# Attention with relative positions, one image at a time: products with v in groups of four key tiles, and x loaded late into a shared buffer

## The chip, the cores and the metric

The kernel runs on one core of one Trainium2 chip. The metric is the time of a run on the device in microseconds. Before the change the median of three runs was 2606.68 us (2600.14 to 2608.02).

## The reference

Eight images of 32 x 32 tokens (T = 1024) with 384 channels go through two layers. The change lies in the first one, cut here to what matters:

```python
# layer 0: x + attention(group_norm(x)), 6 heads of 64
qkv = (x @ qkv_w + qkv_b)                      # per image: q, k, v
attn = einsum('bqd,bkd->bqk', q * SCALE, k)    # 1024 x 1024 per head
attn = attn + rel_h[:, :, :, :, None] + rel_w[:, :, :, None, :]
attn = softmax(attn, axis=-1)
out = einsum('bqk,bkd->bqd', attn, v)
x = x + out @ proj_w + proj_b
# layer 1: t + causal-masked attention over layer_norm(t), then a feed-forward part
t = t + attn1(layer_norm(t))
t = t + ffn(layer_norm(t))
```

## The kernel before, in words

**Order of the whole.** The images are worked one after another. For each, `layer0` makes q, k and v from the group-normed input, the relative-position terms, and then the attention in `attend0_fast`. It returns the residual x and a function `more`, which finishes the projection. `attention1` (the second attention) and, for the first five images, the feed-forward part `ffn` follow. A second, general form of the program (`attend0_general`) stands behind a branch and isn't taken for these data.

**The attention of layer 0.** Scores are made transposed: keys lie on the 128 partitions, the 1024 queries along the free axis. The six heads go in three pairs (`p`), the two heads of a pair being `par` 0 and 1. The keys go in eight tiles of 128 (`c`). For each pair, tile and head, `scores` issues six matmuls (L554) into a PSUM tile of 128 x 1024: the product of k and q, that of the remainders of their rounding (`ks`), and the relative positions (`unit` with `r`), each for two halves of the queries. Their stationary tile is 128*128. ScalarE then takes the exponential into a page `pr` (L558). A page is a buffer of 128 x 1024 floats; a pool of eleven serves all pages, and a pool of eleven larger buffers of 128 x 3080 ("images") serves q, k, v, x and the like.

`values` works on the key tiles in `pending`. First VectorE adds each probability page to the running sum of its head (L567), for the denominator of the softmax. Then TensorE multiplies the probabilities with v (L572): four products per tile, one for each half of the queries and each head. A head has 64 channels, so a product uses 64 of the 128 columns (128*64): head 0 of the pair writes partitions 0 to 63, head 1 partitions 64 to 127. A product in full f32 leaves two records in the profile. Before the change `values` is called whenever two tiles are pending.

**What comes after a pair.** When pair p + 1 is at its second tile, `set_aside` copies the result of pair p to `oT` and folds its sums to 32 columns; at its tile c = 4, right after `values`, `divide` multiplies these into denominators (L602), takes the reciprocal (L580), spreads it (`wide`, L583), transposes it (`rb`, L585) and multiplies `oT` with it (L606). After the last pair `finish` does this without delay: the denominators come from the full sums by matmuls with a matrix of ones (L614), so TensorE needs the last sums of VectorE there; then a transpose (L617), the reciprocal and the spread as before, and a multiply (L620). The projection starts meanwhile on the first two pairs (L659) and is finished by `more` (L664), whose sum with x is on VectorE (L667).

**The residual x.** `residual` loads an image of x by four transfers of 384 KB on SyncE's queue (`load_x`, L105), and GpSimd adds the projection's bias `pb` in a single instruction over 128 x 3072 (L537). For the first image it is called when the binarizing of the feed-forward weights, which is woven into the attention of that image, has run out; in the trace that is in the last pair. For the others it is called at the first pair's second tile.

**What sets the order.** The program is written in the Tile framework. A scheduler with its own costs orders the instructions of each engine, and each engine then runs its own in that order. So the order on TensorE is not quite that of the code: products may be placed before or after a tile's scores, and a group of eight may be divided. The framework adds the waits that the buffers need. The group norm's input of the next image is loaded on SyncE's queue too (L307), behind x; two of the relative-position pages of each pair are worked by `split` (L506 on ScalarE, L507 on VectorE), the third pair's within the attention (`later`).

Of the kernel before, what the change touches and what calls it, by code (L numbers as in the profile page):

```python
# [13 lines left out]
ALU = mybir.AluOpType  # L14
# [3 lines left out]
P = 128  # L18
B, H, W, C = 8, 32, 32, 384
T = H * W  # L20
NJ = T // P
NC = C // P
NH, HD = 6, 64
NPAIR = NH // 2
# [50 lines left out]
def conv_attn_hybrid(  # L75
# [19 lines left out]
    nc = tc.nc  # L95
# [5 lines left out]
    def load_x(pools, b):  # L101
        t = pools.flat(f"x_{b}")[:, : NJ * C].rearrange("p (j c) -> p j c", j=NJ)
        src = x[b].rearrange("(j p) c -> p j c", p=P)
        for q in range(4):
            nc.sync.dma_start(out=t[:, 2 * q : 2 * q + 2, :], in_=src[:, 2 * q : 2 * q + 2, :])  # L105
        return t

    def tile_of(name, shape):
        return const.tile(shape, F32, name=name)
# [3 lines left out]
    pb, b2_sb = tile_of("pb", [P, C]), tile_of("b2_sb", [P, C])  # L113
# [179 lines left out]
    def stages(pools):  # L293
# [100 lines left out]
        def project(w, cols, xT, j, name):  # L394

            ps = pools.o_tile(name)
            for k in range(NC):
                nc.tensor.matmul(ps[:, :C], xT[:, k, ts(j, P)], w[:, k, cols], start=(k == 0), stop=(k == NC - 1))  # L398
            return ps[:, :C]
# [29 lines left out]
        def check(total, reciprocal, i):  # L429
            nc.vector.tensor_reduce(seen[:, 0, i : i + 1], total, AX.X, ALU.add)  # L430
            nc.vector.tensor_reduce(seen[:, 1, i : i + 1], reciprocal, AX.X, ALU.add)


        def layer0(b, xT):
# [99 lines left out]

            def residual():
                xt = load_x(pools, b)
                nc.gpsimd.tensor_tensor(xt, xt, pb.unsqueeze(1).to_broadcast([P, NJ, C]), ALU.add)  # L537
                return xt


# [4 lines left out]
        def attend0_fast(residual, b, sides, v, later):  # L545


            oT = pools.image(f"oT_{b}")

            def scores(p, c, par):  # L550
                sc = pools.s_tile(f"s0_{b}_{p}_{c}_{par}")
                for i, (keys, queries) in enumerate(sides[p][par]):
                    for half in range(2):
                        nc.tensor.matmul(  # L554
                            sc[:, half, :], keys[:, ts(c, P)], queries[:, ts(half, 512)], start=(i == 0), stop=(i == 2)
                        )
                pr = pools.page(f"pr0_{b}_{p}_{c}_{par}")
                nc.scalar.activation(pr, sc.rearrange("p a n -> p (a n)"), AF.Exp)  # L558
                return pr

            def values(p, chunks, sums, avs):
                for c, prs in chunks:
                    for par in range(2):
                        if c == 0:
                            continue
                        prev = first[par] if c == 1 else sums[par]
                        nc.vector.tensor_tensor(sums[par], prev, prs[par], ALU.add)  # L567
                for c, prs in chunks:
                    for half in range(2):
                        for par in range(2):  # L570
                            h = 2 * p + par
                            nc.tensor.matmul(  # L572
                                avs[half][ts(par, HD), :], v[:, c, ts(h, HD)], prs[par][:, ts(half, 512)],
                                start=(c == 0), stop=(c == NJ - 1),
                            )

            def reciprocals(p, tot):

                rt = pools.small.tile([P, 32], F32, tag="rt0", name=f"rt0_{b}_{p}")
                nc.vector.reciprocal(rt, tot)  # L580
                check(tot, rt, b * (NPAIR + 1) + p)
                wide = pools.page(f"wide0_{b}_{p}")
                nc.vector.tensor_copy(wide.rearrange("p (n i) -> p n i", i=32), rt.unsqueeze(2).to_broadcast([P, 32, 32]))  # L583
                rb = pools.page(f"rb0_{b}_{p}")
                nc.vector.transpose(rb, wide)  # L585
                return rb

            def set_aside(p, sums, avs):

                for half in range(2):  # L590
                    nc.scalar.copy(oT[:, p, ts(half, 512)], avs[half])
                few = pools.small.tile([P, 2, 32], F32, tag="few", name=f"few_{b}_{p}")
                for par in range(2):
                    tr = pools.page(f"tr0_{b}_{p}_{par}")
                    nc.vector.transpose(tr, sums[par])
                    nc.vector.tensor_reduce(few[:, par, :], tr.rearrange("p (n i) -> p n i", i=32), AX.X, ALU.add)
                return few

            def divide(p, few):
                den = pools.o_tile(f"den0_{b}_{p}")  # L600
                for par in range(2):
                    nc.tensor.matmul(  # L602
                        den[ts(par, HD), :32], fold.rearrange("p a i -> p (a i)"), few[:, par, :], start=True, stop=True
                    )
                rb = reciprocals(p, den[:, :32])
                nc.vector.tensor_tensor(oT[:, p, :], oT[:, p, :], rb, ALU.mult)  # L606

            def finish(p, sums, avs):

                tr = pools.page(f"tr0_{b}_{p}")  # L610
                for half in range(2):
                    den = pools.o_tile(f"den0_{b}_{p}_{half}")
                    for par in range(2):
                        nc.tensor.matmul(  # L614
                            den[ts(par, HD), :], ones, sums[par][:, ts(half, 512)], start=True, stop=True
                        )
                    nc.vector.transpose(tr[:, ts(half, 512)], den)  # L617
                rb = reciprocals(p, tr.rearrange("p (n i) -> p n i", i=32)[:, :, 0])
                for half in range(2):
                    nc.vector.tensor_tensor(oT[:, p, ts(half, 512)], avs[half], rb[:, ts(half, 512)], ALU.mult)  # L620

            xt, signs = None, binarize(pools) if b == 0 else None
            first = [None, None]
            for p in range(NPAIR):
                sums = [pools.page(f"sum0_{b}_{p}_{par}") for par in range(2)]
                avs = None
                pending = []
                for c in range(NJ):
                    prs = [scores(p, c, par) for par in range(2)]
                    if c == 0:  # L630
                        first = prs
                    if c == 1:
                        if p > 0:
                            few = set_aside(p - 1, *last)
                        if p == 0 and b > 0:
                            xt = residual()
                        avs = [pools.o_tile(f"av0_{b}_{p}_{half}") for half in range(2)]
                    if b == 0 and (p, c) >= (0, 1) and xt is None and next(signs, True):
                        xt = residual()
                    if len(pending) == 2:  # L640
                        values(p, pending, sums, avs)
                        if later:
                            later.pop()()
                        if c == 4 and p > 0:
                            divide(p - 1, few)
                        pending = []
                    pending.append((c, prs))
                values(p, pending, sums, avs)
                last = (sums, avs)
            finish(NPAIR - 1, *last)  # L650


            begun = []
            for j in range(4):
                if j % 2 == 0:
                    both = pools.s_tile(f"pj_{b}_{j}")
                begun.append(both[:, j % 2, :C])
                for k in range(2):
                    nc.tensor.matmul(begun[j], oT[:, k, ts(j, P)], wproj_sb[:, k, :], start=(k == 0), stop=False)  # L659

            def more(j):
                if j < 4:
                    ps = begun[j]
                    nc.tensor.matmul(ps, oT[:, 2, ts(j, P)], wproj_sb[:, 2, :], start=False, stop=True)  # L664
                else:
                    ps = project(wproj_sb, slice(0, C), oT, j, f"pj_{b}_{j}")
                nc.vector.tensor_tensor(xt[:, j, :], ps, xt[:, j, :], ALU.add)  # L667

            return xt, more
# [287 lines left out]
    with ExitStack() as scope:  # L957
        pools = Pools(scope, tc, "f")
# [43 lines left out]
```

## Time and profile before

| | before |
|---|---|
| median of the runs | 2606.68 us |
| profiled execution, span | 2599.5 us |
| granted TensorE clock, mean | 0.996 |
| busy: TensorE | 2521.0 us, 97% |
| busy: VectorE | 1619.4 us, 62% |
| busy: ScalarE | 1157.0 us, 45% |
| busy: GpSimd | 115.5 us, 4% |
| products with v, L572 | 1536 records, 359.7 us |
| scores, L554 (three groups) | 2304 records, 746.9 us |
| running sums, L567 (two groups) | 336, 406.9 us |
| adds of the bias to x, L537 | 8, 60.9 us, 7.6 us each |

In the profile PE stands for TensorE, DVE for VectorE, ACT for ScalarE, POOL for GpSimd and SP for SyncE. A group of instructions is given by its line, engine and operation and by the tiles that it writes and reads, with numbers left out of their names: `f_s` is a score tile, `f_av` a product with v, `f_pr` a page of probabilities, `f_sum` a running sum, `f_den` denominators, `f_x` an image of x. After the bar come the busy time and the mean of one instruction in nanoseconds, and then the idle time of the engine just before the group, with what ended it. The timeline view lists stretches of like instructions with their start, the time from first start to last end, and their number. Matmuls are pipelined and each record overlaps the next, so the time that one costs is read from start to start, not from its length.

### The profile page before, as it was taken

To read this page: it belongs to the slowest core of one execution; us is meant where nothing else is said; L and a number is where in the kernel's file an instruction comes from. 1 tells how busy PE (TensorE), PEld (TensorE's weight loads), DVE (VectorE), ACT (ScalarE), POOL (GpSimd) and SP (SyncE) were. 2 spreads that over 40 slices of the span, in tenths; PEclk is the share of its full clock that TensorE was granted. 3 is DMA by queue.
4 is the path that set the end of the run, shared out by engine and by line. 5 is a ranking of instruction groups with operands and counts; after the bars stand their busy time and mean duration, and the time that the engine had idled before them with its cause. 6 is when DMAs were issued, how large, how long until landed. Compare 5 with 4: busy or idle time off the path is not lost. (4 is left out here: it accounts for less than half of the span.)

```text
span 2599.5 us, 25162 instructions
## 1 busy us (share of the span) xinstructions
PE 2521.0 (97%) x9538; PEld 1508.4 (58%) x9538; DVE 1619.4 (62%) x2407; ACT 1157.0 (45%) x1513; POOL 115.5 (4%) x106
## 2 busy tenths in 40 slices
PE   7999998999999999999999999999999999999998
PEld 4555685555765556755557555576555555555554
DVE  5895468763587644786545776347864486538652
ACT  4641377421666314764127643156641264127420
POOL 1000002000001000010000100000100010001000
PEclk9999999999999999999999999999999999999999
DMA  6431106011042101150110601003200240015000
GB/s 167 147 146 61 37 1 170 1 61 37 1 117 54 49 13 37 41 130 1 61 37 1 170 1 61 6 31 91 80 25 1 67 104 1 25 39 131 1 1 26
DMA packets 148993, 144.72 MB, mean 56 GB/s; under 512 B 107264, under 2 KB 129664, under 8 KB 147328
## 3 DMA queue, kind: packets, MB, share of 16 engines
q1 hardware_dynamic: 142928, 119.36, 16.4%
q0 software_dynamic: 2880, 23.59, 2.6%
q8 instruction: 77, 1.26, 0.2%
q10 hardware_dynamic: 3056, 0.08, 0.1%
q14 instruction: 52, 0.43, 0.1%
HBM read 75.38 MB, written 42.47 MB: 45 GB/s over the span
## 5 line engine op out<-in xcount | busy, mean ns | idle before, releaser
L558 ACT ACTIVATE f_pr<-f_s 128x1024 f32<-128x1024 f32 x384 | 393.0, 1027 | 403.2 <-PE f_s L554 370.3
L567 DVE TENSOR_TENSOR f_sum<-f_sum,f_pr 128x1024 f32<-128x1024 f32 x288 | 349.0, 1244 | 147.0 <-ACT f_pr L558 145.6
L572 PE MATMUL f_av<-f_pr,f_v 128*64 128x512 f32 x1536 | 359.7, 599 | 0.0
L554 PE MATMUL f_s<-f_q,f_k 128*128 128x512 f32 x768 | 258.5, 418 | 21.8 <-ACT f_pr L558 14.9
L388 PE MATMUL f_qk<-f_gnT,wqkv_sb 128*128 128x512 f32 x576 | 261.5, 598 | 8.2 <-DVE f_k L456 5.6
L554 PE MATMUL f_s<-f_q,f_ks 128*128 128x512 f32 x768 | 245.3, 401 | 0.0
L554 PE MATMUL f_s<-f_r,unit 128*128 128x512 f32 x768 | 243.1, 398 | 0.0
L572 PEld LDWEIGHTS f_av<-f_pr,f_v 128*64 128x64 f32 x1536 | 103.2, 136 | 202.8 <-issue 195.0
L507 DVE TENSOR_TENSOR f_r<-f_near,f_r 32x1024 fp32r<-32x1024 f32 x96 | 193.7, 2017 | 29.0 <-ACT f_r L506 26.3
L554 PEld LDWEIGHTS f_s<-f_q,f_k 128*128 128x128 f32 x768 | 125.8, 189 | 137.9 <-issue 50.3
L762 PE MATMUL f_s<-f_q,f_lnT 128*128 128x512 f32 (+3 forms) x576 | 201.4, 491 | 0.0
L776 PE MATMUL f_av<-f_v,f_pr 128*128 128x385 f32 x576 | 194.5, 486 | 0.0
L388 PEld LDWEIGHTS f_qk<-f_gnT,wqkv_sb 128*128 128x128 f32 x576 | 108.0, 191 | 124.3 <-issue 114.0
L554 PEld LDWEIGHTS f_s<-f_q,f_ks 128*128 128x128 f32 x768 | 145.6, 190 | 35.9
L554 PEld LDWEIGHTS f_s<-f_r,unit 128*128 128x128 f32 x768 | 145.8, 190 | 34.8
L776 PEld LDWEIGHTS f_av<-f_v,f_pr 128*128 128x128 f32 x576 | 108.6, 190 | 78.6 <-issue 11.5
L506 ACT CAST f_r<-f_near 32x1024 fp32r<-32x1024 f32 x96 | 145.9, 1520 | 2.3
L398 PE MATMUL f_v<-wqkv_sb,f_gnT 128*128 128x384 f32 x384 | 129.4, 490 | 10.5 <-ACT f_v L512 8.3
L762 PEld LDWEIGHTS f_s<-f_q,f_lnT 128*128 128x128 f32 x576 | 100.1, 190 | 67.7 <-issue 43.5
L877 DVE TENSOR_REDUCE am<-f_h 128x1 f32<-128x1024 f32 (+2 forms) x80 | 71.6, 946 | 96.6 <-ACT f_h L870 96.6
L770 ACT ACTIVATE f_pr<-f_s 128x1024 f32<-128x1024 f32 (+3 forms) x64 | 41.7, 651 | 202.0 <-DVE f_s L767 202.0
L870 ACT ACTIVATE f_h<-f_y,b_sb 128x256 f32<-128x256 f32 x240 | 100.8, 472 | 67.0 <-PE f_y L866 67.0
(163 smaller groups left out, 3360.6 us busy)
## 6 DMA issues: line engine op xcount, KB each, us to landing
f_far<-f_far SPq DMA_DIRECT2D x48, 512.0 KB, 2.9
f_ks<-f_k SPq DMA_DIRECT2D x96, 256.0 KB, 5.1
f_gnT<-in_xT SPq DMA_DIRECT2D x24, 512.0 KB, 4.5
f_near<-f_far SPq DMA_DIRECT2D x96, 128.0 KB, 3.9
f_x<-in_x SPq DMA_DIRECT2D x32, 384.0 KB, 6.4
out_y<-f_x SPq DMA_DIRECT2D x32, 384.0 KB, 3.8
f_w1a<-w1s POOLq DMA_DIRECT2D x5, 1536.0 KB, 7.2
f_w2a<-w2s POOLq DMA_DIRECT2D x5, 1536.0 KB, 6.6
```

Source lines behind the costliest of these rows:

```text
L388: nc.tensor.matmul(ps[:, half, :], w[:, k, cols], xT[:, k, ts(half, 512)], start=(k == 0), stop=(k == NC - 1),)
L398: nc.tensor.matmul(ps[:, :C], xT[:, k, ts(j, P)], w[:, k, cols], start=(k == 0), stop=(k == NC - 1))
L506: nc.scalar.copy(dst[ts(hi, 32)], src)
L507: nc.vector.tensor_tensor(dst[ts(lo, 32)], src, dst[ts(hi, 32)].bitcast(F32), ALU.subtract)
L554: nc.tensor.matmul(sc[:, half, :], keys[:, ts(c, P)], queries[:, ts(half, 512)], start=(i == 0), stop=(i == 2))
L558: nc.scalar.activation(pr, sc.rearrange("p a n -> p (a n)"), AF.Exp)
L567: nc.vector.tensor_tensor(sums[par], prev, prs[par], ALU.add)
L572: nc.tensor.matmul(avs[half][ts(par, HD), :], v[:, c, ts(h, HD)], prs[par][:, ts(half, 512)], start=(c == 0), stop=(c == NJ - 1),)
L762: nc.tensor.matmul(sc[:, half, lo:], xT[:, c // 4, k, ts(c % 4, P)], q[:, half, k, lo:], start=(k == 0), stop=(k == NC - 1),)
L776: nc.tensor.matmul(av[:, : C + 1], prs[c][:, ts(j - c, P)], v[:, c, :], start=(c == 0), stop=(c == j))
L870: nc.scalar.activation(pairs[i][:, m, :, :], ps[:, ts(i % 2, 256)].rearrange("p (j q) -> p j q", j=2), AF.Identity, bias=b1_sb[:, m : m + 1],)
L877: nc.vector.tensor_reduce(am[:, i, n - 1 : n], pairs[i][:, cuts[n - 1] : cuts[n], :, :], AX.XYZ, ALU.max, apply_absolute_value=True)
```

## The change

From the second image on, `values` is called for four key tiles together, so TensorE changes less often between scores and products with v. That keeps the probabilities of four tiles alive, which takes more pages than there are. So x is no longer loaded at the start of the attention: its buffer (`room`) holds three pages of probabilities of each four tiles until the last pair, and x is loaded into it there, behind the first products of that pair. To have the add of the bias begin with the first transfer, GpSimd's single instruction becomes four, one for each transfer; this holds for the first image too. For the first image the rest stays as it was.

```diff
             def residual():
                 xt = load_x(pools, b)
-                nc.gpsimd.tensor_tensor(xt, xt, pb.unsqueeze(1).to_broadcast([P, NJ, C]), ALU.add)
+                for i in range(4):
+                    part = xt[:, 2 * i : 2 * i + 2, :]
+                    nc.gpsimd.tensor_tensor(part, part, pb.unsqueeze(1).to_broadcast([P, 2, C]), ALU.add)
                 return xt
...
-                pr = pools.page(f"pr0_{b}_{p}_{c}_{par}")
+                i = 2 * (c % 4 - 1) + par
+                if room and 0 <= i < 3 and (p, c) < (NPAIR - 1, 4):
+                    pr = room[0][:, i, :]
+                else:
+                    pr = pools.page(f"pr0_{b}_{p}_{c}_{par}")
...
             first = [None, None]
+            room = [pools.image(f"room_{b}")] if b > 0 else []
+            n_av = 4 if room else 2
...
-                        if p == 0 and b > 0:
-                            xt = residual()
...
-                    if len(pending) == 2:
+                    if len(pending) == n_av:
                         values(p, pending, sums, avs)
+                        if room and p == NPAIR - 1:
+                            xt = residual()
```

In the changed kernel the lines move down: scores are L556, exponentials L564, sums L573, products L578, the last denominators L620, the adds of the bias L539.

## The prediction
> **What bounds the kernel now.** I read the page's busy shares first, then its chain, then the groups of the attention that the change touches.
>
> ```profile
> PE 2521.0 (97%) x9538; PEld 1508.4 (58%) x9538; DVE 1619.4 (62%) x2407; ACT 1157.0 (45%) x1513; POOL 115.5 (4%) x106
> ...
> PE f_s L554 8%; PE f_av L572 5%; PE f_s L762 3%; PE f_av L776 3%; PE f_qk L388 2%; PE f_v L398 2%; PE f_q L724 2%; PE f_pj L398 1%; PE f_pj L659 1%; ACT f_r L506 0%; PE f_rel L479 0%; PE f_pj L664 0%; DMA f_near<-f_far 0%; DMA f_far<-f_far 0%; PE f_pt L300 0%; DMA f_ks<-f_k 0%
> ...
> L558 ACT ACTIVATE f_pr<-f_s 128x1024 f32<-128x1024 f32 x384 | 393.0, 1027 | 403.2 <-PE f_s L554 370.3
> L567 DVE TENSOR_TENSOR f_sum<-f_sum,f_pr 128x1024 f32<-128x1024 f32 x288 | 349.0, 1244 | 147.0 <-ACT f_pr L558 145.6
> L572 PE MATMUL f_av<-f_pr,f_v 128*64 128x512 f32 x1536 | 359.7, 599 | 0.0
> L554 PE MATMUL f_s<-f_q,f_k 128*128 128x512 f32 x768 | 258.5, 418 | 21.8 <-ACT f_pr L558 14.9
> ```
>
> TensorE is 97% busy and the chain is TensorE almost throughout. ScalarE's exponentials (L558) and VectorE's running sums (L567) idle because they wait for scores. So a microsecond counts if it is TensorE's own, or a wait of TensorE. The change takes no matmul away; what it can save on TensorE is the cost of switching between scores (stationary tile 128*128, L554) and products with v (128*64, L572). The timeline of image 2 shows that cost (columns: start, length, work):
>
> ```profile
> 805.47 0.63 PE L554 MATMUL f_s<-f_q,f_ks 128*128 128x512 f32 x2
> ...
> 805.93 0.62 PE L554 MATMUL f_s<-f_r,unit 128*128 128x512 f32 x2
> 806.49 3.65 PE L572 MATMUL f_av<-f_pr,f_v 128*64 128x512 f32 x16
> ...
> 810.07 0.74 PE L554 MATMUL f_s<-f_q,f_k 128*128 128x512 f32 x2
> ...
> 810.64 0.62 PE L554 MATMUL f_s<-f_q,f_ks 128*128 128x512 f32 x2
> ```
>
> From start to start a pair of score matmuls takes 805.93 − 805.47 = 0.46 us (0.465 over many), but 0.56 going into the burst of products, and 0.57 for the first pair after it. The burst itself takes 3.58 for eight products (16 records). Image 0 has one burst of twice that:
>
> ```profile
> 101.98 7.09 PE L572 MATMUL f_av<-f_pr,f_v 128*64 128x512 f32 x32
> 109.00 0.73 PE L554 MATMUL f_s<-f_q,f_k 128*128 128x512 f32 x2
> ```
>
> 7.02 us for sixteen, so (7.02 − 3.58)/8 = 0.43 per product and 3.58 − 8 × 0.43 = 0.14 per burst. A burst costs 0.10 + 0.11 + 0.14 = **0.35 us** over its arithmetic. Those 0.43 hold for products that run in pairs, one in each column half; one alone does not share:
>
> ```profile
> 443.18 1.07 PE L572 MATMUL f_av<-f_pr,f_v 128*64 128x512 f32 x2
> 444.19 0.73 PE L554 MATMUL f_s<-f_q,f_k 128*128 128x512 f32 x2
> ...
> 447.77 3.65 PE L572 MATMUL f_av<-f_pr,f_v 128*64 128x512 f32 x14
> 451.35 0.73 PE L554 MATMUL f_s<-f_q,f_k 128*128 128x512 f32 x2
> ```
>
> One product takes 1.01, and seven take 3.58, as long as eight. Splitting a group at an odd place costs 2 × 0.43 = 0.86 us besides the switch.
>
> The other half of the change is where x is loaded and gets its bias on GpSimd (L537). In image 2 that happens early, with a VectorE instruction blocked beside it; in image 0, where x comes late, in the last pair:
>
> ```profile
> 793.76 8.50 POOL L537 TENSOR_TENSOR f_x<-f_x,pb 128x3072 f32<-128x3072 f32 x1 [37.54 <-DMA f_x<-in_x]
> ```
>
> ```profile
> 188.60 7.21 POOL L537 TENSOR_TENSOR f_x<-f_x,pb 128x3072 f32<-128x3072 f32 x1 [68.83 <-DMA f_x<-in_x]
> ...
> 189.10 13.47 DVE L567 TENSOR_TENSOR f_sum<-f_sum,f_pr 128x1024 f32<-128x1024 f32 x6
> ...
> 201.49 3.06 PE L614 MATMUL f_den<-f_sum,ones 128*64 128x512 f32 x8 [0.94 <-DVE f_sum L567]
> ```
>
> Six sums took 13.47 there; at the pitch of sums back to back, 1.14, they take 6.9. They were not done when TensorE came to the denominators (L614). Image 2 has the same stretch without the add:
>
> ```profile
> 901.00 1.89 PE L614 MATMUL f_den<-f_sum,ones 128*64 128x512 f32 x8
> ```
>
> No wait there. From the last score pair to the denominators it is 4.92 us in image 0 and 3.80 elsewhere, from there to the projection (L659) 2.99 and 1.82: the late add cost image 0 (4.92 − 3.80) + (2.99 − 1.82) = **2.3 us**.
>
> **What the Trainium skill says.** "TensorEngine Tiling (Array Packing)", Key Properties: changing the tiling mode drains the TensorE, and tiles operate independently. The trace agrees on both: 0.35 us per burst, and 0.43 instead of about 0.9 per product in pairs. "SBUF — State Buffer", Who interferes with whom: a VectorE instruction with two SBUF inputs contends with a GpSimd instruction that reads SBUF; the port pair is locked for the whole instruction, and DMA does not contend. The trace agrees: one TENSOR_TENSOR of L507 took 7.59 us beside the add of image 2 and 1.99 a little later, while the one-input copies of L484, beside another GpSimd instruction (L915), took 0.69 as everywhere.
>
> **The change, part by part.**
>
> *Fewer bursts.* The order of the instructions on TensorE, per image from the second on: before, 13 bursts (one of 1, one of 7, eleven of 8); after, 9: of 1, 2, 13, three full of 16, then 16, 3 and 13 in the last pair. Four switches go: −4 × 0.35 = −1.4. The first pair's split at an odd place (1 and 7; now 1, 2, 13) is there before and after; the last pair's, 3 and 13, is new: +0.86. Net **−0.5 per image, −3.8 for seven**; from rounding and scatter, −3 to −5. Were the odd split free: −9.8. Image 0 keeps its bursts.
>
> *Later sums and probabilities.* Probabilities are kept for four tiles, three of them in the room's buffer. The waits that the changed ScalarE, exponentials included, gets for pages and room are all on VectorE and TensorE work that lies several us back (the tightest, the last exponential of an image on the last pair's rb, has about 6 us of slack). Cost 0; bound 0 to 0.3 per image.
>
> *x off the early place.* The add no longer blocks L507 by about 5.6 us in seven images. I find no TensorE wait beside these, so 0.
>
> *x into the last pair.* The load is queued on SyncE behind the last reader of the room. With t = 0 at the start of the last pair's first burst of 16 products: that reader is the eleventh product, t = 5.4 with its wait; image 0's landings were 3.4, 4.5, 5.5, 6.5 after the first issue, so parts arrive at t = 8.8 to 11.9. GpSimd needs 6.8 us for the whole (fastest row of L537 is 6.76), in four parts 1.7 each, from about 9.5 on. In the same stretch: denominators of the pair before come at t = 6.9 (after 16 products, where before it was after 8), then in VectorE's order a reciprocal, a spread copy, eight sums, one transpose, one multiply. Without GpSimd: start 7.3, reciprocal and copy 1.3 with gaps, nine two-input instructions × 1.14–1.2 = 10.4, transpose 1.2: done at 20.2. TensorE: scores resume at 7.1, three products at 10.1, 24 scores from 12.0, thirteen products at 17.8, and these, (13 + 1) × 0.43 less the overlap, end at about 23.5, where the denominators need the last sums. Slack 3.4. GpSimd's 6.8 all lock out two-input instructions; the transpose (1.2) can run beside them, which leaves 5.6: VectorE is done at 24.2 to 25.0 with starts and handovers. **TensorE then waits about 0.8 us per image, × 7 = +5.6.** Bounds: 0 (add in the gaps of VectorE) and 3.5 (image 0's 2.3, with up to four handovers of 0.3 more). x itself is ready at t < 20; its reader, the residual sum (L667), comes 6 us after the denominators (908.98 in image 2): no wait.
>
> *Four parts in image 0.* The add starts with the first landing, about 3 us earlier, and can overlap the transpose (1.24): **−1.2**, between 0 and −2.
>
> Sum: −3.8 + 5.6 − 1.2 = +0.6; with 2606.7 as base and half a microsecond for the waits above, **2608**.
>
> **Rivals.**
>
> (A) *VectorE becomes the bound in the last pair, as in image 0.* For it: image 0's 13.47 for six sums, and the changed order makes VectorE start later still, since it idles behind the reciprocal for a burst of sixteen. GpSimd's neighbouring instructions can also run through without VectorE (L919 waited up to 2.55 instead of 0.61 beside L915). Against: the parts wait for their own landings, and a sum may go in between. Then 7 × 2.3 to 7 × 3.5 instead of 5.6, and no gain in image 0: −3.8 + 16 to 24.5 = +12 to +21, so 2619 to 2627; I take 2621. Slower.
>
> (B) *The add is hidden.* GpSimd begins while VectorE waits for the reciprocal, or stands in its shadow. Against: the landings (t ≥ 8.8) come after the reciprocal (7.3). Then −3.8 − 1.2: 2602, within 0.3%. If, besides, the odd split costs little because the products before and after fill in, −9.8 − 1.2: **2596**, faster. The 1.01 for one product speaks against.
>
> (C) *The new place of x delays DMAs behind it on SyncE's queue*, the next image's group-norm input. Image 0 has that sequence already: x at 181.88, the next input's loads (L307) at 195.66. In image 2 these land by 903.4 and are first read at 927.8, so 20 us of delay would go unseen. 2608 as well, at worst 2612.
>
> **How the numbers follow.** Forecast, with the small forms of B and C: 0.56. A: 0.26, of which 0.25 passes +0.3% (7.8 us, 2614.5). B with free odd splits: 0.18, of which 0.17 passes −0.3% (2598.9). Thus faster 0.18, same 0.56, slower 0.26. The range: 2596 to 2622 holds the forecast with its bounds, half of B's far form and half of A or more, about 0.8.
>
> **What would show it.** Bursts of x32 records of L572 of 7.0 us in images 1 to 7, each with 0.56 before and 0.57 after. One burst in each last pair of x6 records at about 1.9 us. L507's mean down from 2017 ns to about 1600. L537 (L539 after) x32, about 1.7 us each or over 2 where it waits, in the last pair, with sums of over 2 us beside it. At the denominators (L620 after) an idle time with VectorE's sum as releaser, seven times: about 0.8 each means right, over 2 means A, none B. Wrong altogether if TensorE waits for a probability in the middle of a pair, or if x arrives after the residual sum wants it.

## The result, and the profile after

The changed kernel took 2605.64 us (median, 2603.68 to 2607.35) where the kernel before took 2607.35 beside it. The ratio of the means is 0.9999 with an interval of 0.9980 to 1.0019; in a second, longer comparison it was 1.0004 (0.9994 to 1.0014). The total shows no change that can be told from zero, as forecast. The longer executions mostly are those with the lower granted TensorE clock: in the largest comparison the kernel before had a mean span of 2605.6 us at 0.995 and of 2597.5 at 0.998.

The total hides opposite terms of a few us, so most of what follows uses finer measures from the trace, as means over images 1 to 7:

- **T**, the time of one image from its 21st score matmul (shortly before the first product) to its first projection matmul. (It isn't the number of tokens that the reference calls T.) In image 2 of the changed kernel it runs from 789.07 to 900.97. T repeats: 111.92 in both profiles of the changed kernel, 110.41 and 110.52 in those of another version; single images of a run lie up to 1 us apart.
- **T33**, the same from the 33rd score matmul. Much of T's scatter lies ahead of it: a wait of 0.5 us at the 31st score matmul, which comes in two to five of the seven images of every version but one, and a slower start of the scores. T33 is the better measure of differences under 0.3 us.
- **E**, the end alone, from the first product of an image's last burst to its first projection matmul. It was 5.30 in every one of images 1 to 7 before.

| | before | after |
|---|---|---|
| T, images 1 to 7 | 111.45 us | 111.92 us |
| T33, images 1 to 7 | 106.80 us | 107.24 us, 107.30 in the second profile |
| image 0, 63rd score matmul to projection | 109.33 us | 108.24 us |
| inferred total of the attentions, by T | | 7 x 0.47 − 1.09 = +2.2 us |

The profiled spans differ by more, 2599.5 and 2605.6. But executions of the changed kernel had spans of 2597.5 to 2607.1 in the second comparison, and the rest of that difference lies between the attentions, where the order of TensorE is the same. T also leaves out the end of the program: from the last matmul to the end of the span it is 9.0 to 9.5 us in the profiles of the kernel before and of two versions without the room, and 7.0 to 7.7 in those of all versions with it. The cause of that is open; it would take 1.3 to 1.5 us off the inferred total.

The page after: the busy shares, then the same groups as before (columns: busy us, mean ns, idle time just before, releaser).

```profile
PE 2523.1 (97%) x9538; PEld 1514.0 (58%) x9538; DVE 1612.0 (62%) x2407; ACT 1155.8 (44%) x1513; POOL 138.1 (5%) x130
...
L573 DVE TENSOR_TENSOR f_sum<-f_sum,f_pr 128x1024 f32<-128x1024 f32 x225 | 297.2, 1354 | 15.4 <-ACT f_pr L564 13.4
...
L507 DVE TENSOR_TENSOR f_r<-f_near,f_r 32x1024 fp32r<-32x1024 f32 x96 | 152.6, 1589 | 51.8 <-ACT f_r L506 49.0
...
L539 POOL TENSOR_TENSOR f_x<-f_x,pb 128x768 f32<-128x768 f32 x32 | 83.1, 2624 | 1237.3 <-DMA f_x<-in_x 849.4
```

TensorE is as busy as before. L507 fell from 2017 ns to 1589: nothing blocks it any more. The block went to the sums: this group has 1354 ns where it had 1244, and all sums together take 431 us where they took 407. Each part of the add takes 2.6 us. The timeline of image 2's last pair shows the mechanism (rows of several engines in order of time; other rows between them are left out).

```profile
880.37 2.14 SPq L105 DMA_DIRECT2D f_x<-in_x  x4
881.89 0.26 PE L608 MATMUL f_den<-few,fold 128*64 128x32 f32 x4
882.22 0.36 DVE L586 RECIPROCAL rt<-f_den 128x32 f32<-128x32 f32 x1 [6.26 <-PE f_den L608]
...
883.88 10.69 POOL L539 TENSOR_TENSOR f_x<-f_x,pb 128x768 f32<-128x768 f32 x4 [126.66 <-PE f_s L556]
885.05 1.93 PE L578 MATMUL f_av<-f_pr,f_v 128*64 128x512 f32 x6
885.61 1.70 DVE L573 TENSOR_TENSOR f_sum<-f_sum,f_pr 128x1024 f32<-128x1024 f32 x1
887.24 2.85 DVE L612 TENSOR_TENSOR f_oT<-f_oT,f_rb 128x1024 f32<-128x1024 f32 x1
890.01 9.04 DVE L573 TENSOR_TENSOR f_sum<-f_sum,f_pr 128x1024 f32<-128x1024 f32 x5
892.69 5.79 PE L578 MATMUL f_av<-f_pr,f_v 128*64 128x512 f32 x25
897.97 0.64 PE L620 MATMUL f_den<-f_sum,ones 128*64 128x512 f32 x1
898.32 0.59 PE L578 MATMUL f_av<-f_pr,f_v 128*64 128x512 f32 x1
898.45 2.59 PE L620 MATMUL f_den<-f_sum,ones 128*64 128x512 f32 x7
...
900.97 3.49 PE L667 MATMUL f_pj<-wproj_sb,f_oT 128*128 128x384 f32 x10
```

GpSimd's four parts and VectorE's two-input instructions take turns: each starts about 2.8 us after the one before it on its engine, so the add lasts 10.69. Parts that run alone, in a version below, take 1.85 and start 1.81 apart, about 7.3 for four. The last sum ends at 890.01 + 9.04 = 899.05. The denominators begin at 897.97, beside the thirteenth product (its second record at 898.32), but those of the second head need that last sum: inside the x7 the trace has one start-to-start gap of 0.65 us, to 899.11; without the add (below) this gap is 0.42. The whole wait is larger, since the first denominators come a little late as well. E is 8.26 to 8.32 in these images and 7.87 without the add: a wait of **0.42**.

A second wait was not foreseen. In image 2 after:

```profile
794.66 1.08 PE L578 MATMUL f_av<-f_pr,f_v 128*64 128x512 f32 x4
...
796.08 2.10 ACT L506 CAST f_r<-f_near 32x1024 fp32r<-32x1024 f32 x1
...
798.10 0.62 PE L556 MATMUL f_s<-f_r,unit 128*128 128x512 f32 x2
798.21 1.94 ACT L564 ACTIVATE f_pr<-f_s 128x1024 f32<-128x1024 f32 x2
...
799.28 0.73 PE L556 MATMUL f_s<-f_q,f_k 128*128 128x512 f32 x2 [0.56 <-ACT f_pr L564]
```

and the same place before:

```profile
797.11 3.65 PE L572 MATMUL f_av<-f_pr,f_v 128*64 128x512 f32 x14
...
798.31 2.02 ACT L506 CAST f_r<-f_near 32x1024 fp32r<-32x1024 f32 x1
800.68 0.74 PE L554 MATMUL f_s<-f_q,f_k 128*128 128x512 f32 x2
```

ScalarE's fourth cast for the third pair's positions (L506, 2 us) lay beside a burst of seven products; it cost nothing. With the products put off, scores stand there instead. There are two score tiles, both wait for an exponential behind the cast, and TensorE waits: 0.70 to 0.95 us from start to start, instead of 0.23, in every image from the second on. This is at the 49th score matmul (the 55th in the last two images) and makes **0.55** as a mean.

### The profile page after: what moved, and what is told of

The parts are those of the page before. It is cut to its first block, busy times and chain, and to the rows that moved or that the text cites. A ratio compares the mean times of both kernels' runs of the same rounds, so it can differ in the third digit from the quotient of the medians.

```text
span 2605.6 us, 25084 instructions
## 1 busy us (share of the span) xinstructions
PE 2523.1 (97%) x9538; PEld 1514.0 (58%) x9538; DVE 1612.0 (62%) x2407; ACT 1155.8 (44%) x1513; POOL 138.1 (5%) x130
## 4 chain that ended last, share of the span: by engine, by line
PE 73%; DVE 9%; ACT 9%; issue 4%; DMA 3%; SPq 1%; POOL 0%; ACTq 0%; DVEq 0%; POOLq 0%
PE f_s L556 15%; PE f_av L578 10%; PE f_s L770 7%; PE f_av L784 7%; PE f_qk L388 7%; PE f_y L874 6%; PE f_v L398 5%; PE f_q L732 5%; PE f_y L913 4%; ACT f_r L506 3%; DVE f_sum L573 3%; PE f_pj L398 2%; PE f_pj L667 2%; PE f_rel L479 1%; PE f_pt L300 1%
## 5 line engine op out<-in xcount | busy, mean ns | idle before, releaser
L564 ACT ACTIVATE f_pr<-f_s 128x1024 f32<-128x1024 f32 x279 | 284.6, 1026 | 208.8 <-PE f_s L556 189.1
L573 DVE TENSOR_TENSOR f_sum<-f_sum,f_pr 128x1024 f32<-128x1024 f32 x225 | 297.2, 1354 | 15.4 <-ACT f_pr L564 13.4
L578 PE MATMUL f_av<-f_pr,f_v 128*64 128x512 f32 x1116 | 305.2, 599 | 0.0
L556 PE MATMUL f_s<-f_q,f_k 128*128 128x512 f32 x768 | 256.1, 415 | 23.0 <-ACT f_pr L564 16.5
L556 PE MATMUL f_s<-f_q,f_ks 128*128 128x512 f32 x768 | 244.8, 400 | 0.0
L556 PE MATMUL f_s<-f_r,unit 128*128 128x512 f32 x768 | 242.7, 397 | 0.0
L556 PEld LDWEIGHTS f_s<-f_q,f_k 128*128 128x128 f32 x768 | 124.5, 189 | 123.2 <-ACT f_pr L564 46.9
L507 DVE TENSOR_TENSOR f_r<-f_near,f_r 32x1024 fp32r<-32x1024 f32 x96 | 152.6, 1589 | 51.8 <-ACT f_r L506 49.0
L578 PEld LDWEIGHTS f_av<-f_pr,f_v 128*64 128x64 f32 x1116 | 86.5, 137 | 140.6 <-issue 138.8
L556 PEld LDWEIGHTS f_s<-f_q,f_ks 128*128 128x128 f32 x768 | 145.3, 189 | 35.5
L556 PEld LDWEIGHTS f_s<-f_r,unit 128*128 128x128 f32 x768 | 145.6, 190 | 34.4
L564 ACT ACTIVATE f_room<-f_s 128x1024 f32<-128x1024 f32 x105 | 107.5, 1026 | 128.2 <-PE f_s L556 127.9
L539 POOL TENSOR_TENSOR f_x<-f_x,pb 128x768 f32<-128x768 f32 x32 | 83.1, 2624 | 1237.3 <-DMA f_x<-in_x 849.4
L506 ACT CAST f_r<-f_near 32x1024 fp32r<-32x1024 f32 x96 | 146.3, 1524 | 2.3
```

The source lines that it names most:

```text
L506: nc.scalar.copy(dst[ts(hi, 32)], src)
L507: nc.vector.tensor_tensor(dst[ts(lo, 32)], src, dst[ts(hi, 32)].bitcast(F32), ALU.subtract)
L556: nc.tensor.matmul(sc[:, half, :], keys[:, ts(c, P)], queries[:, ts(half, 512)], start=(i == 0), stop=(i == 2))
L578: nc.tensor.matmul(avs[half][ts(par, HD), :], v[:, c, ts(h, HD)], prs[par][:, ts(half, 512)], start=(c == 0), stop=(c == NJ - 1),)
```

## The experiments

Each ratio is to the kernel before, timed beside it. Together the experiments measure the terms one by one.

**The add of the bias taken away.** Images 1 to 7 lack the projection's bias here.

```diff
-                for i in range(4):
+                for i in range(4 if b == 0 else 0):
```

> The changed kernel with GpSimd's add of the bias left out for images 1 to 7 (x is loaded as before, the bias of the projection is missing from these images). Measure: time from an image's 21st score matmul to its first projection matmul; 111.45 us before the change and 111.92 after, means over images 1 to 7. Theory: VectorE's last sums come about 0.44 us too late for the denominators because the add locks them out; without it the 0.65 us gap among the last-denominator matmuls falls to 0.2 and each image gets 0.4 to 0.5 shorter (111.45), in all 3 us or 0.12%. Rival: VectorE is late because it idles behind the reciprocal, not because of the add; then the gap stays and nothing changes.

T 111.34, so −0.58; T33 106.85, so −0.39 to −0.45; E 7.87 in every image, so −0.42. The gap of 0.65 among the denominators is 0.42, not the expected 0.2: two records, one in each column half, start together every 0.42, so 0.21 is only their mean. Ratio 0.9989 (0.9977 to 1.0002). In the timeline VectorE is at leisure (image 2):

```profile
882.07 0.36 DVE L586 RECIPROCAL rt<-f_den 128x32 f32<-128x32 f32 x1 [6.26 <-PE f_den L608]
...
892.51 5.79 PE L578 MATMUL f_av<-f_pr,f_v 128*64 128x512 f32 x25
893.67 1.22 DVE L573 TENSOR_TENSOR f_sum<-f_sum,f_pr 128x1024 f32<-128x1024 f32 x1 [0.18 <-ACT f_pr L564]
...
897.72 0.59 PE L620 MATMUL f_den<-f_sum,ones 128*64 128x512 f32 x1
898.14 0.59 PE L578 MATMUL f_av<-f_pr,f_v 128*64 128x512 f32 x1
898.14 2.30 PE L620 MATMUL f_den<-f_sum,ones 128*64 128x512 f32 x7
900.38 5.11 PE L667 MATMUL f_pj<-wproj_sb,f_oT 128*128 128x384 f32 x15
```

The reciprocal still comes 6.26 us late, but the last sum ends at 894.89. The first denominators that need it start at 898.57 (inside the x7), 3.7 us later. The wait is the add's; the late reciprocal alone makes none.

**The kernel before, with x called for in the last pair.**

```diff
-                        if p == 0 and b > 0:
-                            xt = residual()
...
                     if len(pending) == 2:
                         values(p, pending, sums, avs)
+                        if b > 0 and (p, c) == (NPAIR - 1, 4):
+                            xt = residual()
```

> The kernel before, products by two tiles, with only x's place changed: loaded at tile 4 of the last pair, the add in four parts. Theory (the add alone is what VectorE can't hide): denominators wait for the sums, by 0.4 to 1.5 us per image as the burst ahead of them is shorter than after the change: 111.45 becomes 112.0 to 113.0. Image 0 gains the 1.1 us that it gained in the changed kernel, since its add is in four parts too. Rival (the late start behind a burst of 16 is needed for the wait): 111.45 stays, no wait at the denominators.

T 111.21, T33 106.76, E 5.30 in every image, so no wait; ratio 1.0002 (0.9989 to 1.0015). But this didn't test what it was for: x had a free buffer of its own, and the scheduler still placed the load at the start of the attention. In image 2 the add ran from 795.45:

```profile
795.45 10.85 POOL L539 TENSOR_TENSOR f_x<-f_x,pb 128x768 f32<-128x768 f32 x4 [39.21 <-DMA f_x<-in_x]
```

So it is the kernel before with an add in four parts, and shows two things: image 0 gains 1.0 us (109.33 to 108.34) by the parts alone, and early parts neither cost nor save anything in the other images: T33 is 0.04 under before, and T's −0.24 lies ahead of the 33rd score matmul.

**The late x by itself.** The same question, with the load forced behind the room's readers: the changed kernel with groups of two throughout.

```diff
-            n_av = 4 if room else 2
+            n_av = 2
...
-                        if room and p == NPAIR - 1:
+                        if room and (p, c) == (NPAIR - 1, 4):
                             xt = residual()
```

> The changed kernel's place of x with the order of before: products by two tiles throughout (13 bursts, order on TensorE as before), x loaded after the products of tiles 2 and 3 of the last pair into the room, which forces the late load; in the run meant for this the scheduler took the load early, as its buffer was free. 111.21 per image with the early place and four parts. Theory (the late add alone makes the sums late): VectorE loses about 5.4 us behind the reciprocal where some 3.6 to 4 us of idle time and 1.1 us of lead stand, so the denominators wait 0.5 to 1.5 us: 111.7 to 112.7. Rival (it takes the later start behind a burst of 16): no wait, 111.2.

T 112.21, one us over the 111.21 of the early place; T33 107.64, 0.88 over it; E 6.17, 0.87 over it. Ratio 1.0011 (1.0000 to 1.0022). Image 2:

```profile
888.70 10.20 POOL L539 TENSOR_TENSOR f_x<-f_x,pb 128x768 f32<-128x768 f32 x4 [134.58 <-PE f_s L556]
...
894.34 9.04 DVE L573 TENSOR_TENSOR f_sum<-f_sum,f_pr 128x1024 f32<-128x1024 f32 x5
...
902.76 2.60 PE L620 MATMUL f_den<-f_sum,ones 128*64 128x512 f32 x8
```

The last sum ends at 903.38 and the eight denominators take 2.60 instead of 1.89. The late add makes the wait with groups of two as well: the burst of sixteen isn't needed for it. The wait is even longer, 0.87 against 0.42 by E; TensorE comes to the denominators without an odd split here, which probably makes the difference, but wasn't tried apart.

**The add in one instruction.** The changed kernel with the single add of before.

```diff
-                for i in range(4):
-                    part = xt[:, 2 * i : 2 * i + 2, :]
-                    nc.gpsimd.tensor_tensor(part, part, pb.unsqueeze(1).to_broadcast([P, 2, C]), ALU.add)
+                nc.gpsimd.tensor_tensor(xt, xt, pb.unsqueeze(1).to_broadcast([P, NJ, C]), ALU.add)
```

> The changed kernel with the add of the bias in one instruction, as before. Theory: the add starts after the last landing, some 3 us later, and no transpose lies beside it, so the sums end 1.2 us later: the wait at the denominators grows from 0.45 to about 1.6, 113.1 per image, and image 0 loses its 1.1: 9.5 us over the changed kernel, ratio to the kernel before about 1.0035. Rival (parts cost as much in handovers as they gain): 111.9 per image.

T 113.06, E 9.46, image 0 back at 109.36; ratio 1.0043 (1.0029 to 1.0057). The four parts are worth 1.14 us per image by T where x is late, 1.17 by E. In image 2 the single add starts at 890.10, after the last landing, and five sums beside it take 12.41:

```profile
890.10 7.19 POOL L537 TENSOR_TENSOR f_x<-f_x,pb 128x3072 f32<-128x3072 f32 x1 [132.85 <-DMA f_x<-in_x]
...
890.51 12.41 DVE L571 TENSOR_TENSOR f_sum<-f_sum,f_pr 128x1024 f32<-128x1024 f32 x5
```

**Products for each tile by itself.** The kernel before with 21 bursts instead of 13, to measure the switch.

```diff
-                    if len(pending) == 2:
+                    if len(pending) == (1 if b > 0 else 2):
```

> The kernel before with the products taken for each key tile by itself from the second image on: 21 bursts per image instead of 13, none at an odd place. Theory (a switch costs 0.35 us): +8 x 0.35 = +2.8 per image, less up to 0.86 as no odd split is left: 113.4 to 114.3 per image against 111.45; +14 to +20 us in all, ratio 1.0052 to 1.0076. Rival (switches hide behind TensorE's waits for ScalarE): 111.4.

T 112.63, ratio 1.0028 (1.0018 to 1.0039): slower, though less than expected. The burst itself is as priced (image 2):

```profile
815.94 0.62 PE L554 MATMUL f_s<-f_r,unit 128*128 128x512 f32 x2
816.49 1.94 PE L572 MATMUL f_av<-f_pr,f_v 128*64 128x512 f32 x8
818.36 0.72 PE L554 MATMUL f_s<-f_q,f_k 128*128 128x512 f32 x2
818.92 0.63 PE L554 MATMUL f_s<-f_q,f_ks 128*128 128x512 f32 x2
```

0.55 into it, 1.87 for four products, 0.56 after it; less 0.465, 4 x 0.43 and 0.465 this makes 0.33. From T it is (1.18 + 0.86)/8 = 0.26. What the expectation left out is the wait for a score tile at the 31st score matmul, about 0.5 us in images 1, 6 and 7 of the kernel before, so 0.2 as a mean; a burst covers it here. T33 (107.68, +0.88) doesn't contain this wait. With the three products that come ahead of the 33rd score matmul here, and the odd product that is gone, it makes (0.88 + 3 x 0.43 + 0.43)/8 = 0.325. So a switch costs **0.33**, and T alone shows it too small.

**The last tiles from last to first.** The changed kernel, one burst of 16 in place of 3 and 13; the flag that ends an accumulation goes with the new last product.

```diff
-                for c, prs in chunks:
+                for c, prs in reversed(chunks) if p == NPAIR - 1 and len(chunks) == 4 and chunks[0][0] else chunks:
                     for half in range(2):
```

> The changed kernel with the products of the last four tiles of the last pair taken from the last tile to the first, so that none can be taken early: one burst of 16 in place of bursts of 3 and 13. Theory (VectorE's sums are the bound at the denominators): TensorE is 1.2 us earlier there and waits 1.2 longer, 111.9 per image stays within 0.2. Rival (TensorE's odd split is what costs): -0.86 - 0.35 = 1.2 us less per image, 110.7, in all -8.5 us, ratio 0.9967.

The same, with the add left out as above (again no bias in images 1 to 7):

> The changed kernel with the last four tiles' products from last to first (one burst of 16) and with the add of the bias left out for images 1 to 7 (their bias is missing). Theory: with the add away VectorE no longer bounds the denominators, and the 1.2 us of the odd split and of the switch that a wait swallowed in the run with the add now show: 111.74 - 0.45 - 1.2 = 110.1 to 110.3 per image. Rival (order of the products never mattered): 111.3, as without the add alone.

T 111.74 with the add (ratio 1.0004, 0.9995 to 1.0014) and 111.31 without (0.9991, 0.9983 to 1.0000). The first looks like the theory confirmed, the second says it isn't: without the add the gain should have shown, and T is that of the old order (111.34). The trace of the second, image 2, gives the reason:

```profile
890.76 7.41 PE L578 MATMUL f_av<-f_pr,f_v 128*64 128x512 f32 x30
890.87 1.02 ACT L564 ACTIVATE f_pr<-f_s 128x1024 f32<-128x1024 f32 x1 [0.37 <-PE f_s L556]
...
897.68 0.59 PE L620 MATMUL f_den<-f_sum,ones 128*64 128x512 f32 x1
898.01 0.59 PE L578 MATMUL f_av<-f_pr,f_v 128*64 128x512 f32 x1
```

The burst now begins with the last tile, whose second exponential ends 1.1 us after the first product has started, alone. One column half runs ahead from there on, and two records are left over beside the denominators. E is 9.91, where sixteen products at the rate of before would make 5.30 + 8 x 0.43 = 8.74: 1.17 us lost. The split and its switch lost as much, 0.86 + 0.33. So the edit exchanged one odd start for another, and this pair says nothing on what the odd split costs.

**x before the last pair.** The last pair takes its probabilities from pages and its products by twos; x is loaded at its second tile.

```diff
-                if room and 0 <= i < 3 and (p, c) < (NPAIR - 1, 4):
+                if room and 0 <= i < 3 and p < NPAIR - 1:
...
+                        if room and p == NPAIR - 1:
+                            xt = residual()
                         avs = [pools.o_tile(f"av0_{b}_{p}_{half}") for half in range(2)]
...
-                    if len(pending) == n_av:
+                    if len(pending) == (2 if p == NPAIR - 1 else n_av):
                         values(p, pending, sums, avs)
-                        if room and p == NPAIR - 1:
-                            xt = residual()
```

> As the kernel with twos in the first half of the first pair and in the last pair (110.41 us per image), but with a group of four in the first half of the first pair as in the changed kernel. Ten bursts in both, the same odd splits. Theory: the second burst, of two products instead of seven, no longer covers ScalarE's fourth cast of L506, so scores wait about 0.5 us for a score tile at the 48th score matmul: 110.9 to 111.0 per image, and a gap of 0.7 to 0.95 us there. Rival: that gap is filled elsewhere, 110.4. Against the kernel before: 4.6 us faster, ratio 0.9982 (rival 0.9967).

T 110.81, T33 106.35, with the gap at the 49th score matmul (0.70 to 0.89 us in images 1 to 5, and at the 55th in the last two; the expectation counts from nought). The ratio was 0.9994 (0.9985 to 1.0002), nearer to one than the −5.4 us that T and image 0 would make. The run of fours to the end, timed in the same comparison, has the same excess: −5.4 by T and 0.9990. The cause stays open.

It also prices the odd split. The run without the add has one burst fewer, the same gap in the first pair and no wait at the denominators, but 3 and 13 in the last pair: 106.85 − 106.35 = 0.50 by T33 (0.53 by T), and the saved switch on top makes **0.8 to 0.9** for the odd split. The trace of that run agrees: its three products take 1.86 from start to start (884.89 to 886.75 in image 2), as long as the four in the run of products for each tile by itself, and its E of 7.87 is 0.42 over the 5.30 + 5 x 0.43 = 7.45 of thirteen products at the rate of before.

**Twos in the first half of the first pair too.** On top of the last version:

```diff
-                    if len(pending) == (2 if p == NPAIR - 1 else n_av):
+                    if len(pending) == (2 if p == NPAIR - 1 or (p == 0 and c < 5) else n_av):
```

> Groups of four tiles only from the second half of the first pair to the end of the second; twos in the first half of the first pair and in the last pair; x loaded at the second tile of the last pair, whose probabilities don't use the room. Ten bursts instead of 13 (before) and 9 (after), odd splits as before. Theory (switches cost 0.35 us each, and the gain of the change is eaten by an odd split of 0.86, a wait of 0.44 at the denominators and a wait of about 0.5 for a score tile behind a cast of ScalarE in the first pair): -1.05 per image against the kernel before, 110.4 us per image, -7.4 - 1.1 (image 0) = 8.5 us faster, ratio 0.9967. Rival (fewer bursts save nothing): 111.4 per image, ratio 0.9996. Rival (x in the last pair makes a wait wherever it is put): 110.4 to 111.4 with idle time of TensorE ahead of the denominators.

> The version with fours only from the second half of the first pair to the end of the second, once more beside the two next kernels, to place its total: 110.4 per image, -8.4 us, ratio 0.9968. Rival: the first total was favoured by scatter between executions; then the ratio lies nearer to 0.998 while the time per image stays.

> The changed kernel once more, beside the version with both repairs: 111.9 per image, +2.2 us against the kernel before (+3.3 in images 1 to 7, -1.1 in image 0), ratio 1.0008. Rival: a gain or loss outside the attention that the time per image doesn't show, over 1.002 or under 0.999.

T 110.41 and 110.52; ratios 0.9965 (0.9954 to 0.9977) and 0.9972 (0.9963 to 0.9982), beside 1.0004 for the changed kernel in the second comparison. T33 is 105.81 and 105.83. The gap in the first pair is gone; against the version before this one that is 0.52 to 0.54 per image by T33 (0.3 to 0.4 by T). Image 2 of the second profile, first the place of the gap, where seven products (the last of them in the x7) lie beside the cast again:

```profile
793.51 2.02 ACT L506 CAST f_r<-f_near 32x1024 fp32r<-32x1024 f32 x1
793.65 2.30 PE L578 MATMUL f_av<-f_room,f_v 128*64 128x512 f32 x7
795.88 0.74 PE L556 MATMUL f_s<-f_q,f_k 128*128 128x512 f32 x2
...
859.77 9.27 POOL L539 TENSOR_TENSOR f_x<-f_x,pb 128x768 f32<-128x768 f32 x4 [107.68 <-DMA f_x<-in_x]
...
863.33 1.23 DVE L573 TENSOR_TENSOR f_sum<-f_pr,f_pr 128x1024 f32<-128x1024 f32 x1 [5.07 <-ACT f_pr L564]
...
891.69 3.65 PE L578 MATMUL f_av<-f_pr,f_v 128*64 128x512 f32 x16
892.86 1.22 DVE L573 TENSOR_TENSOR f_sum<-f_sum,f_pr 128x1024 f32<-128x1024 f32 x1 [0.17 <-ACT f_pr L564]
...
895.18 1.89 PE L620 MATMUL f_den<-f_sum,ones 128*64 128x512 f32 x8
```

The add begins where VectorE has 5 us to spare and ends 26 us ahead of the denominators, and these take 1.89 without a wait. This is the best version found, 7 to 9 us under the kernel before.

**Fours to the end.** The version above with the products of the last pair in fours as well, the last four tiles from last to first as in the order experiment:

```diff
-                    if len(pending) == (2 if p == NPAIR - 1 or (p == 0 and c < 5) else n_av):
+                    if len(pending) == (2 if p == 0 and c < 5 else n_av):
```

> Both repairs at once with fours to the end: twos only in the first half of the first pair, then fours; x loaded at the second tile of the last pair, whose probabilities take pages instead of the room; the last four tiles' products from last to first. Eight bursts against 13, odd splits as before. Theory: -5 x 0.35 = -1.75 per image and no wait, 109.7 per image, -12.3 - 1.1 = 13.4 us, ratio 0.9949. Rival (eleven pages are too few in the last pair: ScalarE waits for a page and TensorE for ScalarE): 110.4 per image or more.

T 110.83, T33 106.35, ratio 0.9990 (0.9983 to 0.9996). Two bursts fewer, and 0.52 to 0.54 slower than with twos by T33. Image 2:

```profile
891.62 7.41 PE L578 MATMUL f_av<-f_pr,f_v 128*64 128x512 f32 x30
...
899.39 2.21 PE L620 MATMUL f_den<-f_sum,ones 128*64 128x512 f32 x6
901.53 2.85 PE L667 MATMUL f_pj<-wproj_sb,f_oT 128*128 128x384 f32 x8
```

E is 9.91, as in the run with this order and without the add, so the same 1.17 us are lost; less two switches of 0.33 this makes 0.5, which is the whole difference. None of its score matmuls behind the 33rd waits as much as 0.3 us, so the rival of too few pages doesn't show.

**The terms put together.** Each term has now been read at its own place: a switch 0.325, the odd split 0.86, the wait at the denominators from E (over the like version without the add; with twos, over 5.30), the gap at the score tile 0.55, and 1.17 for the last tile first. Their sums can be held against T33, which was not used for them except for the price of a switch. In us per image, less the 106.80 of the kernel before:

| version | sum of the terms | T33 |
|---|---|---|
| changed kernel | −1.30 + 0.86 + 0.42 + 0.55 = +0.53 | +0.44, +0.50 |
| without the add | −1.30 + 0.86 + 0.55 = +0.11 | +0.05 |
| x early, add in parts, with twos | 0 | −0.04 |
| add in one instruction | −1.30 + 0.86 + 1.59 + 0.55 = +1.70 | +1.62 |
| late x with twos | +0.87 | +0.84 |
| last tile first | −1.63 + 1.17 + 0.41 + 0.55 = +0.50 | +0.48 |
| last tile first, without the add | −1.63 + 1.17 + 0.55 = +0.09 | +0.03 |
| x before the last pair | −0.98 + 0.55 = −0.43 | −0.45 |
| twos first and last | −0.98 | −0.99, −0.97 |
| fours to the end | −1.63 + 1.17 = −0.46 | −0.45 |

All agree within 0.1 us.

## Why the prediction was right, step by step

| step, us per image | predicted | measured |
|---|---|---|
| four switches fewer | −1.4 | −1.3 |
| odd split in the last pair | +0.86 | +0.8 to 0.9 |
| wait at the denominators | +0.8 | +0.42 (E; 0.58 by T) |
| later probabilities, score tile | 0, up to 0.3 | +0.55 |
| sum, images 1 to 7 | +0.26 | +0.47 (T), +0.44 and +0.50 (T33) |
| image 0, whole | −1.2 | −1.1 |

That the sum comes out so near is partly luck: the wait was sized 0.4 too long and the probabilities 0.55 too cheap. And the total alone, with an interval of 0.2% or 5 us to either side, could not have told this from several other sets of terms.

**Fewer bursts** was right in both terms: an odd split eats most of what four switches save. A rival had this split for free; the comparison above refutes it.

**x into the last pair** was right step by step. With the burst's start (874.98) as t = 0: load at 5.4 (predicted 5.4), reciprocal at 7.24 (7.3), VectorE done at 24.1 (24.2 to 25.0). Without the add VectorE leads by 3.7 us (slack 3.4), and the lock takes all of that: the four lengthened instructions lose about 5.4 us together, the predicted 5.6. The Trainium skill, "SBUF — State Buffer", Who interferes with whom, says that only the port pair shared by VectorE and GpSimd makes engines contend, and that it is an exclusive lock; the trace agrees, with starts 2.8 us apart on both engines. The parts were taken too short, 1.7 where one alone takes 1.85. The wait was sized too long, 0.8 against 0.42: the first head's denominators ran beside the odd thirteenth product and were hardly held up, and the second head's were due at 23.75 (as in the run without the add), not at 23.5, so that little more than the time from there to 24.1 is left.

The rival in which VectorE is as late as in image 0 (2.3 us and more per image) needs the single add: that run had T 113.06, 1.6 over before. The four parts keep the change from it. The rival in which the add is hidden shows only where x comes before the last pair. The rival of delayed transfers on SyncE's queue doesn't show: from the second image on, the group norm never waits for its input in the two profiles of the changed kernel, and the residual sum comes 6.2 us after the first projection matmul before and after.

**Later probabilities at cost 0** was wrong, and the 0.55 lies outside the bound of 0.3, though the total hardly shows it. I had looked at the waits of ScalarE for pages, not at what the moved products had covered: the cast of 2 us on ScalarE, with two score tiles between it and TensorE. It also comes near to the sign that the prediction set for being wrong altogether, a wait of TensorE for a probability in the middle of a pair; here it waits for the exponential that frees a score tile.

**x off the early place at 0** was right within 0.1 us: the sums above close without a term for it.

## What to carry to other kernels

Work grouped to save switches also fills the holes of other engines; before moving it, ask at each old place what ran beside it (here a cast of 2 us) and whether the new groups stay even. A GpSimd instruction with VectorE beside it is best put where VectorE idles, well ahead of the next product that waits for VectorE: the same add cost 0.42 us in the last 20 us of an image and nothing visible 25 us earlier.

## What was not expected of the hardware

The add in four parts takes turns with VectorE: 2.8 us for a part that takes 1.85 alone and 2.85 for an instruction of 1.2, 10.7 us in all for about 7.3 us of work. And an odd product shifts its cost rather than paying it at once: the thirteenth ran beside denominators, also of 128*64, that used the other column half (starts at 897.97 and 898.32), but at the end of the denominators one was left to run alone (two starts 0.43 apart in place of two together).
